# Loads and stores of 125 partitions issued as two, of 112 and 13, in a four-layer graph network on one core

## The chip, the cores and the metric

The kernel runs on one core of a Trainium2 chip. The metric is device time in microseconds (us): the median of several executions of the whole program. The profile is one further execution, recorded by the hardware profiler.

## What is computed

The reference applies four layers to x, 3125 nodes with 256 features each, on a graph with 103,125 directed edges (50,000 random pairs in both directions, and a loop at each node, sorted by target). Each layer is

```
xn = layernorm(x)
x = x + gnn(xn, edges) + mix(xn)
x = x + ffn(layernorm(x))          # layers 0, 2, 3 shown alike; layers 1 and 2 feed x itself
```

with other functions in each layer. Layers 0 to 2 use graph attention over (source, target) pairs alone and a linear attention over all nodes as mix. Three parts matter here:

- ffn of layer 0: a router picks the best 2 of 8 experts for each node; an expert is 256 -> 512 (gelu) -> 256; the node gets the two results weighted by a softmax over the two scores.
- gnn of layer 3: every edge has 16 features and a mask of 4 values, so the attention weight of an edge can't be found from its two nodes alone. A softmax over the edges of a target weights the source rows of 8 heads of 32.
- ffn of layer 3: H = gelu(x W1 + b1) with 1024 features, then the most likely of 8 experts, 1024 -> 256, weighted by its probability.

In the result all 3125 x 256 values of x are float32.

## The kernel before

**Layout.** Nodes are cut into NT = 25 tiles of TP = 125, because 3125 = 25 x 125. So x, xn and most tensors with a row for each node have 125 partitions ([125, 25, 256] for x), and so have the transfers that load or store them. Transposed copies (xT) and weights have 128 partitions. GROUPS cuts the 25 tiles in seven groups (4, 4, 4, 4, 3, 3, 3). DRAM tensors of the kernel's own hold what must be read in another order: seg_d, xn_d, y_d, tab (the node table), hid_d.

**Order of work.** Parts outside a `manual_schedule` are put in order by the framework's scheduler, from its own estimate of costs; inside one, TensorE (PE) and VectorE (DVE) keep the order of the code. That is so in the edge loop of layer 3 and in the expert loops of layers 0 and 3 (`edge_attention`, `routed0`, `routed3`). DMAs are issued from the queues of SyncE (SP), ScalarE (ACT) and, for gathers and scatters by index, GpSimd (POOL). Each queue runs in order, and an issue on ACT or POOL stands in line with that engine's computation.

**The start.** `run` loads x with one DMA (L2420), 3.2 MB. `begin_layer` takes the layernorm group by group (L608 to L614) and transposes. `prepare` finds, for each of 3125 target nodes, where its edges begin in a padded list: heads_i (L1342, each partition gets the same 3224 values of row_dst, 1.6 MB), five VectorE reductions over them that count the heads below the partition's first node (L1352, `at`), at_i (L1355), a gather of `segments` by at_i on POOL (L1358), arithmetic on it, and two stores to seg_d (`lo` at L1371, `key` at L1376). Beside it stand checks on the data: dst_i (L1344) and the work on it (dst_f, above, under: L1390 to L1399), and the largest and smallest attention scores (seven pairs of reductions, L1409 and L1410). Their product is `ok` (L1436), and the program branches on it (L2423): with this data it always goes into `layers`.

**Counts and layer 0.** `counts` reads seg_d back ten times as seg_in, 125 x 256 values (L1466), transposes each on TensorE (L1468) and copies it with ACT. From is_lo (L1473) on it builds one-hot matrices and multiplies them (L1501) into a matrix of edge counts. Pieces of layer 0's mix run in between: the addition of bproj to x on POOL (L1528), which the memset of v (L1538) follows, and p_ctx on TensorE (L1540), which reads v. Attention of layers 0 to 2 is then dense, over count tiles (L1670 on VectorE, L1719 and L1770 on TensorE). `gate0` stores the normed rows to xn_d by groups (L2295) and scores the experts. `route` (L2072 to L2143) sorts the pairs of node and expert into tiles of 128. `routed0` gathers xn_d by index (L2353), runs the experts and scatters the results to y_d (L2406); afterwards it loads y_d back, for each group once on SP into xn and once on ACT into xT (L2399, 14 loads, 6.4 MB), and adds each to x (L2401, 50 operations). The next layernorm (L608) follows.

**Layer 3.** `edge_attention` first makes the node table: for each tile TensorE projects, ACT copies to z_row (L1880), and a store of 144.5 KB goes to the table (L1883), 13 on SP and 12 on ACT. The edge loop then has 101 steps of 8 columns of 128 edges. A step loads row (the targets of its edges, the same 1024 int16 values for 125 partitions, 250 KB, L1915, 4 buffers), ef (L1917) and mask (L1919) on SP; gathers eight times 128 table rows by source on POOL (L1925, z_edge, 3 buffers, 806 gathers in all); compares row with the node numbers on VectorE (hot, L1938); sums the target's and the edge's term on TensorE (p_m, L1953), copied to m_sb by ACT (L1955); forms the weights (l, L1968; near_e by ACT, L1976; oh, L1980; z_edge times near_e, L1984) and sums the weighted rows on TensorE (p_acc, L1993). Pieces of layer 3's mix and, for tiles that are done (ENDS), `hidden3` are put between: it computes H and stores it to hid_d with x (L2203, on SP) and with each half row of H (hid_row, L2214, on ACT, 50 stores). `routed3` loads w_d, eight experts of 1024 KB with 128 partitions (L2229), routes, gathers hid_d (hid_tile, L2239), multiplies, scatters to y_d, and copies the first 3125 rows of y_d to `out` with two DMAs from DRAM to DRAM (L2269, one on SP, one on ACT).

The line numbers are those of the kernel before.

Of the kernel before, what the change touches and what calls it, by code (L numbers as in the profile page):

```python
# [21 lines left out]
P = 128  # L22
N = 3125
TP = 125
# [16 lines left out]
NR = EP // ROW  # L41
KEYS = HI * GN
PIECES0 = 107
SC = 8
# [3 lines left out]
HID = 1024  # L48
# [8 lines left out]
class Net:  # L57
# [499 lines left out]
    def setup_dense(self):  # L557
        nc = self.nc
        self.eps10 = self.const.tile([P, 1], F32, name="eps10")
        nc.vector.memset(self.eps10, 1e-10)  # L560
        self.heads = self.const.tile([P, P], F32, name="heads")
        nc.vector.memset(self.heads, 0.0)
        for h in range(4):
            nc.vector.memset(self.heads[32 * h:32 * h + 32, 32 * h:32 * h + 32], 1.0)

    def vec(self, pool, name, rows=C):

# [754 lines left out]
class Dense(Net):  # L1322
# [8 lines left out]
    def prepare(self, pool, xT):  # L1331
# [6 lines left out]
        with ExitStack() as s:  # L1338
            w = s.enter_context(tc.tile_pool(name="prep", bufs=1))
            ps = s.enter_context(tc.tile_pool(name="prepp", bufs=2, space=PSUM))  # L1340
            heads_i = w.tile([TP, NR], I32, name="heads_i")
            nc.sync.dma_start(heads_i, dview(ins["row_dst"], 0, [[0, TP], [1, NR]]))  # L1342
            dst_i = w.tile([P, NE], I32, name="dst_i")
            nc.scalar.dma_start(dst_i, ins["dst_t"])  # L1344
            heads = w.tile([TP, NR], F32, name="heads_f")
# [22 lines left out]
            digit = w.tile([TP, GN, SEG], I32, name="digit")  # L1368
            nc.vector.tensor_scalar(digit, seg[:, :, SEG:], 127, None, op0=OP.bitwise_and)
            nc.vector.tensor_copy(lo, digit)  # L1370
            nc.sync.dma_start(self.seg_d[0], lo)  # L1371
            nc.vector.tensor_scalar(digit, seg[:, :, SEG:], 7, None, op0=OP.logical_shift_right)
            nc.vector.tensor_copy(key, digit)
            nc.vector.scalar_tensor_tensor(key, key, float(GN), rel, op0=OP.mult, op1=OP.add)
            nc.vector.scalar_tensor_tensor(key, key, -127.0, own, op0=OP.add, op1=OP.mult)
            nc.sync.dma_start(self.seg_d[1], key)  # L1376

            found = w.tile([P, 2], F32, name="found")
            nc.vector.memset(found, 0.0)
# [63 lines left out]
    def counts(self, pieces):  # L1443


        nc, tc = self.nc, self.tc
        self.count_d = self.dram.tile([NS, P, N], U8, name="count_d")
        B = 10
        with ExitStack() as s:
            c = s.enter_context(tc.tile_pool(name="cnt", bufs=1))  # L1450
            w = s.enter_context(tc.tile_pool(name="cntw", bufs=2))
            wo = s.enter_context(tc.tile_pool(name="cnto", bufs=1))
            work = pieces(c, wo)
            by_edge = []
            with tc.tile_pool(name="cnti", bufs=1) as wi, tc.tile_pool(name="cntt", bufs=2, space=PSUM) as ps:
                for i, name in enumerate(("lo_t", "key_t")):
                    seg = self.seg_d[i]

                    R = 2 if i else 1
                    t = c.tile([P, NG, 2, R], BF16, name=name)  # L1460
                    for b in range(GN):
                        x = wi.tile([TP, SEG], F32, name="seg_in", bufs=2)
                        nc.sync.dma_start(x, seg[:, b, :])
                        p = ps.tile([P, 2, TP], F32, name="p_t")
                        for i in range(2):
                            nc.tensor.transpose(p[:, i, :], x[:, i * P:(i + 1) * P], self.ident[:TP, :TP])  # L1466
                        for r in range(R):
                            nc.scalar.activation(t[:, b * TP:(b + 1) * TP, :, r], p.rearrange("p i g -> p g i"), AF.Copy)  # L1468
                    by_edge.append(t)
            ps = s.enter_context(tc.tile_pool(name="cntp", bufs=3, space=PSUM))  # L1470
            lo_t, key_t = by_edge
            is_lo = c.tile([P, P, 2 * B], BF16, name="is_lo")
            nc.vector.tensor_copy(is_lo, self.iota[:, :, None].to_broadcast([P, P, 2 * B]))  # L1473
            KP = KEYS + KEYS % 2
            is_key = c.tile([P, KP], BF16, name="is_key")
            nc.vector.tensor_scalar(is_key, self.iota[:, :KP], -127.0, None, op0=OP.add)
            is_pair = is_key.rearrange("p (k r) -> p k r", r=2)
            stage = None
            done, steps = 0, -(-NG // B)
            for g0 in range(0, NG, B):  # L1480
                n = min(B, NG - g0)
                m = 2 * n
                lo = lo_t[:, g0:g0 + n].rearrange("p g i r -> p (g i r)")
                key = key_t[:, g0:g0 + n].rearrange("p g i r -> p (g i) r")
                oh_lo = w.tile([P, P, 2 * B], BF16, name="oh_lo")
                nc.vector.tensor_tensor(oh_lo[:, :, :m], lo[:, None, :].to_broadcast([P, P, m]), is_lo[:, :, :m], OP.is_equal)

                oh_key = w.tile([P, 2 * B, KP], BF16, name="oh_key")
                nc.vector.tensor_tensor(oh_key[:, :m].rearrange("p m (k r) -> p m k r", r=2),
                                        key[:, :, None, :].to_broadcast([P, m, KP // 2, 2]),  # L1490
                                        is_pair[:, None].to_broadcast([P, m, KP // 2, 2]), OP.is_equal)
                at = g0 * GN % 250
                if at == 0:
                    stage = w.tile([P, NS, 250], U8, name="stage")
                for u in range(0, n, 4):
                    m = min(4, n - u)
                    p = ps.tile([P, 4, KEYS], F32, name="p_cnt")
                    for g in range(m):
                        for i in range(2):
                            j = 2 * (u + g) + i  # L1500
                            nc.tensor.matmul(p[:, g, :], oh_lo[:, :, j], oh_key[:, j, :KEYS], start=(i == 0), stop=(i == 1))  # L1501
                    o = stage[:, :, at + u * GN:at + (u + m) * GN]
                    nc.scalar.activation(o.rearrange("p t (g d) -> p t g d", d=GN),
                                         p[:, :m, :].rearrange("p g (t d) -> p t g d", d=GN), AF.Copy)
                if at + n * GN == 250 or g0 + n == NG:
                    d0, nd = g0 * GN - at, at + n * GN
                    nc.sync.dma_start(self.count_d[:, :, d0:d0 + nd].rearrange("t p d -> p t d"), stage[:, :, :nd])
                while done < (g0 // B + 1) * PIECES0 // steps:
                    next(work, None)
                    done += 1  # L1510
            for _ in work:
                pass
# [346 lines left out]
    def edge_attention(self, x, xT, weights, pieces, then):  # L1859
# [10 lines left out]
        with ExitStack() as s:  # L1870
            with ExitStack() as s2:
# [4 lines left out]
                for t in range(NT):  # L1876
# [3 lines left out]
                    nc.scalar.activation(zh[:, :, :D], p[:, :C].rearrange("p (h d) -> p h d", h=H), AF.Copy)  # L1880
                    nc.vector.tensor_copy(rows[:, t, HW:], p[:, C:C + EC])
                    nc.vector.tensor_copy(er[:, t, :], p[:, C + EC:])
                    (nc.scalar if t % 2 else nc.sync).dma_start(table[t * TP:(t + 1) * TP, :], rows[:, t, :])  # L1883
            wz = s.enter_context(tc.tile_pool(name="eg", bufs=3))
            w = s.enter_context(tc.tile_pool(name="ew", bufs=2))
            wt = s.enter_context(tc.tile_pool(name="et", bufs=1))
# [25 lines left out]
            def load(i):  # L1912
                c0, n = steps[i]
                rows[i] = w.tile([TP, SC * P], I16, name="row", bufs=4)
                nc.sync.dma_start(rows[i], dview(dst_d, c0 * P, [[0, TP], [1, SC * P]]))  # L1915
                efs[i] = w.tile([P, 2 * P], F32, name="ef", bufs=4)
                nc.sync.dma_start(efs[i], ins["edge16_s"][i])  # L1917
                masks[i] = w.tile([P, SC, 4], F32, name="mask", bufs=5)
                nc.sync.dma_start(masks[i][:, :n, :], ins["edge4_t"][:, c0:c0 + n, :])  # L1919
# [234 lines left out]
    def hidden3(self, w, ps, x, xn, xT, t0, nt, weights, ones, hid_d):  # L2154


        nc = self.nc
# [42 lines left out]
        nc.vector.tensor_mul(one, one, prob)  # L2200
        share = w.tile([TP, 4], F32, name="share")
        nc.vector.tensor_reduce(share[:, :nt], one, AX.X, OP.add)
        nc.sync.dma_start(hid_d[t0 * TP:(t0 + nt) * TP, HID + 1:].rearrange("(t p) f -> p t f", p=TP), x[:, t0:t0 + nt, :])  # L2203
        yield
        for t in range(nt):
            for i in range(2):
# [4 lines left out]
                nc.scalar.activation(row[:, :512], p[:TP], AF.Copy)  # L2211
                if i:
                    nc.scalar.activation(row[:, 512:], share[:, t:t + 1], AF.Copy)
                nc.scalar.dma_start(hid_d[(t0 + t) * TP:(t0 + t + 1) * TP, i * 512:(i + 1) * 512 + i], row[:, :512 + i])  # L2214
                yield

    def routed3(self, ones, hid_d, out):
# [7 lines left out]
        with ExitStack() as s:  # L2225
# [39 lines left out]
                        products(j - 1)  # L2265

            for i, q in enumerate((nc.sync, nc.scalar)):
                a, b = i * 62 * 25, 62 * 25 if i == 0 else N
                q.dma_start(out[a:b, :].rearrange("(p t) f -> p (t f)", t=25), y_d[a:b, :].rearrange("(p t) f -> p (t f)", t=25))  # L2269

    def matrix_rows(self, pool, name):

# [11 lines left out]
    def gate0(self, ps, x, xn, xT, xn_d, gate, t0, nt):  # L2284
# [5 lines left out]
        with self.tc.tile_pool(name="gate", bufs=1) as w:  # L2290
            v = w.tile([TP, nt, E], F32, name="score")
            for a, na in GROUPS:
                if t0 <= a < t0 + nt:
                    self.layernorm_twice(xn, x, (a, na))
                    nc.sync.dma_start(xn_d.rearrange("(p t) f -> p t f", p=TP)[:, a:a + na, :], xn[:, a:a + na, :])  # L2295
                    for k in range(KC):
                        p = ps.tile([P, 4, P], F32, name="p_o").rearrange("p a b -> p (a b)")
                        for t in range(na):
# [34 lines left out]
    def routed0(self, x, xn, xT, xn_d, gate, weights):  # L2333
# [8 lines left out]
        with ExitStack() as s:  # L2342
# [51 lines left out]
            for t0, nt in GROUPS:  # L2394
                last = t0 if t0 + nt <= KC * N // C else 0
                back = xT.rearrange("p k n -> p (k n)")[:TP, last * C:(last + nt) * C].rearrange("p (t f) -> p t f", f=C)
                for i, y in enumerate((xn[:, t0:t0 + nt, :], back)):
                    own = y_d[i * N:(i + 1) * N, :].rearrange("(p t) f -> p t f", p=TP)
                    (nc.scalar if i else nc.sync).dma_start(y, own[:, t0:t0 + nt, :])  # L2399
                    for t in range(nt):  # L2400
                        nc.vector.scalar_tensor_tensor(x[:, t0 + t, :], y[:, t, :], share[:, i, t0 + t:t0 + t + 1], x[:, t0 + t, :],  # L2401
                                                       op0=OP.mult, op1=OP.add)
# [10 lines left out]
    def run(self, x_in, out):  # L2413
# [3 lines left out]
        x = pool.tile([TP, NT, C], F32, name="x")  # L2417
        xn = pool.tile([TP, NT, C], F32, name="xn")
        xT = pool.tile([P, KC, N], F32, name="xT")
        nc.sync.dma_start(x, x_in.rearrange("(t p) c -> p t c", p=TP))  # L2420
        out_v = out.rearrange("(t p) c -> p t c", p=TP)
        self.begin_layer(x, xn, xT)
        ok = nc.values_load(self.prepare(pool, xT)[0:1, 0:1], min_val=0, max_val=1)  # L2423
# [181 lines left out]
```

## Time and profile before

| | |
|---|---|
| median of 3 runs | 5643.09 us (5640.39 to 5653.39) |
| profiled execution | 5665.5 us, its span 5663.4 us |
| granted TensorE clock, mean | 0.931 |
| busy: PE, VectorE, ScalarE, GpSimd | 87%, 67%, 18%, 18% of the span |
| DMA | 395.78 MB, mean 70 GB/s over the span |

The profiled execution is one of its own and was 22 us longer than the median of the others; times of lines and stretches come from it. A busy share is a mean over stages with different limits: layers 0 to 2 (to about 4300 us) are dominated by VectorE's products (L1670, 1482 us in 1200 instructions) and TensorE's sums over them, the edge loop (4372 to 5430 us) by POOL, TensorE and VectorE side by side. In lists of groups, "out<-in" gives the tensors by the program's names, and "125x256 f32" partitions, elements and type. In a row by stretch of time the last columns are the clock granted to TensorE, the mean busy share of the core's 16 DMA engines and the rate in GB/s.

### The profile page before, as it was taken

What the parts mean: (1) busy time and instruction counts of PE and PEld (TensorE: products, weight loads), DVE (VectorE), ACT (ScalarE), POOL (GpSimd) and SP (SyncE); (2) the same over time, 40 slices, a digit from 0 to 9 for tenths busy, and PEclk for the clock granted to TensorE, in tenths of its full rate; (3) what the DMA queues carried; (4) which work ended last, traced back from release to release, by engine and by line L of the source; (5) the groups of instructions that cost most, each with busy time, mean ns of one, the idle gap of its engine ahead of it and who ended that gap; (6) DMA issues with size and microseconds to landing.
All of it is one profiled execution on the core that took longest, in us unless ns stands there. A gap on an engine that the chain in (4) does not pass through costs nothing. (4 is left out here: it accounts for less than half of the span.)

```text
span 5663.4 us, 66627 instructions
## 1 busy us (share of the span) xinstructions
PE 4906.3 (87%) x24880; PEld 2860.4 (51%) x24880; DVE 3770.6 (67%) x6022; ACT 1040.4 (18%) x1993; POOL 1036.5 (18%) x1183
## 2 busy tenths in 40 slices
PE   3988888879778899989999899979998778988868
PEld 1652234448645433368644433345565556555547
DVE  6789999975455599845443899932222887776743
ACT  1540010011132100110123100023232112332221
POOL 1000000004300000000001100000000777767733
PEclk7999999979889999999889999979999889999979
DMA  2462222232200011111000011020001556656655
GB/s 84 33 62 72 76 63 66 67 109 63 84 29 1 24 34 35 36 40 36 22 1 4 25 33 33 27 70 0 1 0 51 160 158 172 173 173 163 180 161 177
DMA packets 288899, 395.78 MB, mean 70 GB/s; under 512 B 118753, under 2 KB 222578, under 8 KB 287997
## 3 DMA queue, kind: packets, MB, share of 16 engines
q1 hardware_dynamic: 203926, 165.26, 12.0%
q0 software_dynamic: 52496, 167.11, 10.8%
q10 hardware_dynamic: 32148, 59.05, 3.2%
q8 instruction: 203, 3.33, 0.2%
q14 instruction: 126, 1.03, 0.1%
HBM read 345.14 MB, written 49.35 MB: 70 GB/s over the span
## 5 line engine op out<-in xcount | busy, mean ns | idle before, releaser
L1670 DVE SCALAR_TENSOR_TENSOR pt<-q_head,bar,a 128x750 f32<-128x750 f32 (+5 forms) x1200 | 1482.3, 1295 | 80.9 <-PE acc L1775 57.8
L1925 POOL DMA_INDIRECT z_edge<-tab,src_i x806 | 774.2, 961 | 284.0 <-issue 209.2
L1719 PE MATMUL acc<-pt,zs 128*64 128x500 f32 (+2 forms) x2800 | 592.3, 549 | 151.6 <-DVE pt L1670 151.3
L1993 PE MATMUL p_acc<-z_edge,oh 128*125 128x264 f32 x2044 | 539.5, 425 | 101.7 <-DVE z_edge L1984 101.6
L1770 PE MATMUL acc<-pt,zs 128*64 128x375 f32 (+2 forms) x3200 | 605.2, 501 | 25.3 <-DVE pt L1670 24.9
L1993 PEld LDWEIGHTS p_acc<-z_edge,oh 128*125 128x125 f32 x2044 | 418.8, 209 | 202.1 <-DVE z_edge L1984 112.8
L1719 PEld LDWEIGHTS acc<-pt,zs 128*64 128x64 f32 (+1 forms) x2800 | 244.9, 137 | 483.6 <-DVE pt L1670 327.7
L1770 PEld LDWEIGHTS acc<-pt,zs 128*64 128x64 f32 (+1 forms) x3200 | 245.1, 136 | 361.9 <-issue 224.7
L1186 DVE SCALAR_TENSOR_TENSOR x<-p_y,sm,x 125x256 f32<-125x256 f32 x200 | 93.8, 484 | 429.6 <-PE p_y L711 429.6
L1775 PE MATMUL acc<-pt,zs 128*32 128x375 f32 (+2 forms) x3200 | 313.4, 497 | 0.0
L1821 PE MATMUL acc<-zs,pt 128*125 128x257 f32 x1250 | 275.5, 383 | 11.7 <-issue 11.7
L1821 PEld LDWEIGHTS acc<-zs,pt 128*125 128x125 f32 x1250 | 234.7, 189 | 52.5 <-issue 14.5
L1984 DVE TENSOR_TENSOR z_edge<-z_edge,near_e 128x2112 f32<-128x2112 f32 (+1 forms) x101 | 236.4, 2341 | 18.6 <-ACT near_e L1976 18.5
L1181 ACT ACTIVATE h<-p_tr,bn 128x500 f32<-128x500 f32 (+1 forms) x224 | 161.5, 722 | 361.7 <-PE p_tr L711 361.7
L711 PE MATMUL p_y<-w_L_ffn_Wo,h 128*125 128x256 f32 x800 | 203.7, 387 | 0.0
L1670 DVE SCALAR_TENSOR_TENSOR pt<-q_all,bar,a 128x500 f32<-128x500 f32 (+3 forms) x175 | 118.9, 681 | 122.7 <-PE acc L1821 120.2
L711 PE MATMUL p_tr<-h,w_L_ffn_W 128*128 128x500 f32 (+1 forms) x448 | 192.7, 554 | 7.7 <-ACT h L1181 4.6
L1617 POOL MEMSET es<- 128x4 f32 (+2 forms) x4 | 1.4, 346 | 1053.7 <-PE acc L1775 725.2
L711 PE MATMUL p_tr<-xT,w_L_ffn_W 128*128 128x500 f32 (+1 forms) x448 | 193.9, 556 | 0.0
L2309 POOL CAST one_e<-one 125x96 bf16<-125x96 f32 (+1 forms) x2 | 2.1, 1050 | 1024.4 <-DVE one L648 1024.4
L1775 PEld LDWEIGHTS acc<-pt,zs 128*32 128x32 f32 (+1 forms) x3200 | 85.0, 109 | 203.1 <-issue 201.8
L711 PEld LDWEIGHTS p_y<-w_L_ffn_Wo,h 128*125 128x125 f32 x800 | 144.9, 187 | 73.5 <-ACT h L1181 27.2
(504 smaller groups left out, 7014.9 us busy)
## 6 DMA issues: line engine op xcount, KB each, us to landing
row<-dst_row SPq DMA_DIRECT2D x101, 250.0 KB
a<-count_d SPq DMA_DIRECT2D x96, 203.1 KB
a<-count_d SPq DMA_DIRECT2D x96, 187.5 KB
a<-count_d SPq DMA_DIRECT2D x144, 93.8 KB
ef<-in_edge_s SPq DMA_DIRECT2D x101, 128.0 KB
z_edge<-tab,src_i POOLq DMA_INDIRECT x806, 3.0
count_d<-stage SPq DMA_DIRECT2D x12, 781.2 KB
q_head<-q_g ACTq DMA_DIRECT2D x24, 375.0 KB
```

What stands on the lines that cost most here:

```text
L711: self.nc.tensor.matmul(p, a, b, start=(i == 0), stop=(i == len(pairs) - 1))
L1181: nc.scalar.activation(o[:, m, :n], p[:, :n], AF.Relu, bias=b[:, e, m:m + 1], scale=g[:, e, m:m + 1])
L1186: nc.vector.scalar_tensor_tensor(x[:, t0 + t, :], q, wf[:, t, e:e + 1], x[:, t0 + t, :], op0=OP.mult, op1=OP.add)
L1670: self.nc.vector.scalar_tensor_tensor(pt[:K, :n], q, bar, a[:K, :n], op0=OP.max, op1=OP.mult)
L1719: nc.tensor.matmul(acc[64 * i:64 * i + 64, :b1 - b0], zs[:K, t, z:z + 64], pts[i][:K, b0:b1], start=(t == 0), stop=(t == NS - 1))
L1770: nc.tensor.matmul(acc[i // 2][64 * (i % 2):64 * (i % 2) + 64, b, :b1 - b0], zs[:K, t, i * W:i * W + 64], pts[i][:K, b0:b1], **st)
L1775: nc.tensor.matmul(acc[2][32 * i:32 * i + 32, b, :b1 - b0], zs[:K, t, z:z + 32], pts[i][:K, b0:b1], **st)
L1821: nc.tensor.matmul(acc[i], pt[:K, i * TP:(i + 1) * TP], zs[:K, t, :C + 1], start=(t == 0), stop=(t == NS - 1))
L1925: nc.gpsimd.indirect_dma_start(out=zs[i][:, j, :], out_offset=None, in_=table, in_offset=bass.IndirectOffsetOnAxis(ap=src[:, c0 + j:c0 + j ...
L1984: nc.vector.tensor_mul(zh, zh, weight[:, :, :, None].to_broadcast([P, n, H, D + 1]))
L1993: nc.tensor.matmul(acc[t], ohs[i, t][:, k - a, :], zs[i][:, k - c0, :HW], start=(k == cols[t][0]), stop=(k == cols[t][1] - 1))
L2309: nc.gpsimd.tensor_copy(ones[:, 0, ts, :], one1)
```

## The change

A helper, `part_dma`, issues one transfer of 125 partitions as two on the same queue: partitions 0 to 111 and 112 to 124. It is used for the row heads, both stores to seg_d and the loads of seg_in, the stores of xn_d, the loads of y_d in `routed0`, the stores of the node table, the load of row in the edge loop, and the stores of hid_d. Besides: x is loaded by groups, alternately on SP and ACT (so its one DMA becomes 14); of the five pairs of seg_in loads for each of two tensors the second and the fourth go to ACT's queue instead of SP's; and the copies to `out` become two of 1536 rows (24 rows to a piece, 64 pieces) and one of the last 53 rows on POOL's queue, instead of 1550 and 1575 rows (62 and 63 pieces of 25).

```diff
+    def part_dma(self, queue, out, in_):
+
+        queue.dma_start(out[:112], in_[:112])
+        queue.dma_start(out[112:TP], in_[112:TP])
...
-            nc.sync.dma_start(heads_i, dview(ins["row_dst"], 0, [[0, TP], [1, NR]]))
+            self.part_dma(nc.sync, heads_i, dview(ins["row_dst"], 0, [[0, TP], [1, NR]]))
...
-            nc.sync.dma_start(self.seg_d[0], lo)
+            self.part_dma(nc.sync, self.seg_d[0], lo)
...
-            nc.sync.dma_start(self.seg_d[1], key)
+            self.part_dma(nc.sync, self.seg_d[1], key)
...
-                        nc.sync.dma_start(x, seg[:, b, :])
+                        self.part_dma(nc.scalar if b % 2 else nc.sync, x, seg[:, b, :])
...
-                    (nc.scalar if t % 2 else nc.sync).dma_start(table[t * TP:(t + 1) * TP, :], rows[:, t, :])
+                    self.part_dma(nc.scalar if t % 2 else nc.sync, table[t * TP:(t + 1) * TP, :], rows[:, t, :])
...
-                nc.sync.dma_start(rows[i], dview(dst_d, c0 * P, [[0, TP], [1, SC * P]]))
+                self.part_dma(nc.sync, rows[i], dview(dst_d, c0 * P, [[0, TP], [1, SC * P]]))
...
-        nc.sync.dma_start(hid_d[t0 * TP:(t0 + nt) * TP, HID + 1:].rearrange("(t p) f -> p t f", p=TP), x[:, t0:t0 + nt, :])
+        self.part_dma(nc.sync, hid_d[t0 * TP:(t0 + nt) * TP, HID + 1:].rearrange("(t p) f -> p t f", p=TP), x[:, t0:t0 + nt, :])
...
-                nc.scalar.dma_start(hid_d[(t0 + t) * TP:(t0 + t + 1) * TP, i * 512:(i + 1) * 512 + i], row[:, :512 + i])
+                self.part_dma(nc.scalar, hid_d[(t0 + t) * TP:(t0 + t + 1) * TP, i * 512:(i + 1) * 512 + i], row[:, :512 + i])
...
-                a, b = i * 62 * 25, 62 * 25 if i == 0 else N
-                q.dma_start(out[a:b, :].rearrange("(p t) f -> p (t f)", t=25), y_d[a:b, :].rearrange("(p t) f -> p (t f)", t=25))
+                a, b = i * 1536, (i + 1) * 1536
+                q.dma_start(out[a:b, :].rearrange("(p t) f -> p (t f)", t=24), y_d[a:b, :].rearrange("(p t) f -> p (t f)", t=24))
+            nc.gpsimd.dma_start(out[3072:N, :], y_d[3072:N, :])
...
-                    nc.sync.dma_start(xn_d.rearrange("(p t) f -> p t f", p=TP)[:, a:a + na, :], xn[:, a:a + na, :])
+                    self.part_dma(nc.sync, xn_d.rearrange("(p t) f -> p t f", p=TP)[:, a:a + na, :], xn[:, a:a + na, :])
...
-                    (nc.scalar if i else nc.sync).dma_start(y, own[:, t0:t0 + nt, :])
+                    self.part_dma(nc.scalar if i else nc.sync, y, own[:, t0:t0 + nt, :])
...
-        nc.sync.dma_start(x, x_in.rearrange("(t p) c -> p t c", p=TP))
+        x_v = x_in.rearrange("(t p) c -> p t c", p=TP)
+        for i, (t0, nt) in enumerate(GROUPS):
+            self.part_dma(nc.scalar if i % 2 else nc.sync, x[:, t0:t0 + nt, :], x_v[:, t0:t0 + nt, :])
```

## The prediction

> **What bounds the kernel now.** I read the page first, then busy time, granted clock and DMA share by stretches of time, then the timeline at each place where the diff touches a load, and last the waits of POOL. The page says that TensorE is busy for most of the span, so a faster transfer gains only where all engines stand and wait for it:
>
> ```profile
> PE 4906.3 (87%) x24880; PEld 2860.4 (51%) x24880; DVE 3770.6 (67%) x6022; ACT 1040.4 (18%) x1993; POOL 1036.5 (18%) x1183
> ```
>
> Three such places exist. The first two show in the stretches (columns: stretch, its length, busy us of PE, PEld, DVE, ACT, POOL, granted clock, DMA share, GB/s); the third row group is a load of 128 partitions for comparison:
>
> ```profile
> 10.00:20.00 10.00, 0.00 (x0) 0.00 (x0) 1.17 (x2) 0.00 (x0) 0.00 (x0) 1.00 0.34 121
> 20.00:26.00 6.00, 0.00 (x0) 0.00 (x0) 0.00 (x0) 0.00 (x0) 0.00 (x0) 1.00 0.34 121
> ...
> 1540.00:1550.00 10.00, 0.00 (x0) 0.00 (x0) 3.90 (x10) 0.00 (x0) 0.00 (x0) 0.50 0.32 132
> 1550.00:1560.00 10.00, 0.00 (x0) 0.00 (x0) 3.25 (x8) 0.00 (x0) 0.00 (x0) 0.50 0.32 131
> ...
> 5468.00:5472.00 4.00, 0.00 (x0) 0.00 (x0) 3.90 (x21) 0.60 (x1) 0.00 (x0) 0.50 1.03 375
> 5472.00:5476.00 4.00, 0.30 (x3) 0.43 (x4) 3.87 (x15) 0.00 (x0) 0.00 (x0) 0.50 1.07 386
> ```
>
> At 10 to 26 us x is loaded, at 1540 to 1560 the results y_d of layer 0's experts: both have 125 partitions, both keep the 16 DMA engines busy to 0.32 to 0.34, close to 5/16 = 0.31, and move 121 to 132 GB/s. The load of w_d, with 128 partitions, fills all of them and moves 375 to 386. In the first two places TensorE stands and VectorE works at most 4 of 10 us. The timeline (start, us, engine, line, operation, count, idle before and its releaser) shows where these waits end:
>
> ```profile
> 33.69 0.75 DVE L608 BATCH_NORM_STATS2 bn_st<-x 125x6 f32<-125x256 f32 x2 [22.50 <-DMA x<-in_x]
> ...
> 1538.97 1.67 DVE L2401 SCALAR_TENSOR_TENSOR x<-xn,share,x 125x256 f32<-125x256 f32 x4 [21.18 <-DMA xn<-y_d]
> ...
> 1585.16 0.75 DVE L608 BATCH_NORM_STATS2 bn_st<-x 125x6 f32<-125x256 f32 x2
> ...
> 4360.33 0.38 ACT L1880 ACTIVATE z_row<-p_z 125x256 f32<-125x256 f32 x1 [1.73 <-DMA tab<-z_row]
> ...
> 4371.64 0.25 SPq L1915 DMA_DIRECT2D row<-dst_row  x1
> ```
>
> VectorE starts on x at 33.69; the last x update of layer 0 ends at 1585; and after the last row of layer 3's node table (4360) nothing moves until its stores have landed (4371.6). Then the edge loop of layer 3 begins, over 1000 us that belong to POOL's gathers:
>
> ```profile
> L1925 POOL DMA_INDIRECT z_edge<-tab,src_i x806: 940/946/1947, 4372.4 to 5429.1; - x162
> ...
> POOL z_edge L1925 <- issue: 209.2, 686, 0.5
> POOL z_edge L1925 <- PE p_acc L1993: 49.5, 37, 6.2
> ```
>
> One gather is 0.946 us and 0.30 of issue, so 806 need 1.25 x 806 = 1007 of the 1058 us; 49.5 us are waits for a buffer that PE's sums free.
>
> **What the skill says.** "DMA: Bandwidth & Descriptors", section "Why a DMA increments its semaphore by 16 and not by 1": a hardware-issued DMA runs on k engines, k the largest number up to 16 that divides the outermost sizes of both sides. 125 gives 5, 112 gives 16, 13 gives 13. The trace agrees: 0.34 against 1.03 above. The same page, "Issuing engines are not separate dma queues": a second issuing queue saves only issue time. So the alternation of SP and ACT earns little by itself; the trace has 0.25 to 0.7 us for an issue. No page prices the waits that doubled DMAs bring.
>
> **The change, part by part.** After a split an engine carries at most 7 + 1 = 8 partitions instead of 25, so a lone transfer can be 3.1 times as fast, up to the 375 to 386 GB/s seen. Each split adds one issue of 0.25 to 0.4 us on its queue. The compiled order also shows that SP's and ACT's DMAs take eight semaphores in turn, and that a DMA waits for the one eight before it; twice the DMAs means half the reach.
>
> *Start.* x is 3.2 MB: 31 us at 121 GB/s and after the change about 10 at 325 (16 engines at the 20 GB/s that each shows here), but VectorE needs only the first groups. They land near 5.5 us (issue 0.7 to 2.5, then 1 MB of groups 0 and 1 mixed at 325 GB/s = 3.1). Groups then come every 1.5 us, while VectorE takes 25 us for seven. The row heads (1.6 MB, 5 us) follow at about 18 and are needed at 30. Before, VectorE worked from 33.69 to at_i at 78.2. The compiled order moves 4.6 us of dst work (L1390, L1397 to L1399, hidden under x until now, because dst_i's load sits behind x on ACT's queue and three activations) into this chain, and 2.3 us of reductions out of it: 5.5 + 44.5 + 4.6 - 2.3, with some waits 53.7, so at_i is 24.5 earlier. The gathers of segments and the work to seg_key take 12 + 13.7 us as before. But the compiled order puts six of seven pairs of L1409/L1410 behind seg_key, where only one was: with TensorE cold (0.8 us a matmul at first) I count 9 us, of which the seg_key store hid 2.6 before. So the branch comes near 95 instead of 110.9: **gain 15** (11 to 22; more if the reductions slip forward, less if the groups queue on each other).
>
> *Start of the counts.* Ten seg_in loads become twenty, four of them on ACT. Each transfer shrinks by under 1 us, but POOL's addition of bproj (L1528, 13.8 us, on which v's memsets and TensorE's p_ctx wait) now has its load behind a seg_in on ACT, and a waiting seg_in holds ACT's ek, v and key_t copies. **-1** (-5 to +4).
>
> *Stores of xn_d and of seg_d.* The last xn_d store is issued by 1241, the gather that reads it starts at 1278 behind the routing (L2072 to L2143): nothing; if that cover went, 3 us.
>
> *Results of layer 0.* 6.4 MB in 14 loads, and 2.6 MB of weights ahead of them on the same engines from 1518. At 350 GB/s 9.0 MB take 26 us, so the last lands near 1546. VectorE needs 50 x 0.41 = 20.5 us, from a first arrival near 1532: it ends at 1552 instead of 1585.2, and VectorE itself is late next. **Gain 32** (26 to 37; the low end is 300 GB/s and stalls on the eight semaphores).
>
> *Node table.* 25 stores, 3.6 MB, ran at 109 GB/s for 37 us against TensorE's 27. After the split TensorE paces them (1.08 us a tile, two stores each); the last is issued at 4360.1 and lands 2.5 later, as POOL's scatters do: 4362.7 instead of 4371.6. **Gain 8.5** (5 to 9.5).
>
> *Edge loop.* The loads of row (250 KB, 101 times) and the stores of hid_d (25.6 + 15.6 MB in all) lie on five engines that the gathers also need; spread out, a gather's worst landing (7.5 us, median 3.0) shrinks, and with it part of the 49.5 us. Against it: 50 more issues of 0.26 us on ACT, 110 on SP, which is idle. The trace doesn't show how much of the 49.5 is late landing: between 10 gained and 6 lost, **gain 4**.
>
> *End.* hid_d's last stores shared five engines with w_d; at 5476 to 5480 the rate dips to 159 GB/s. That is 1.3 MB lost, 3.5 us at 380: **gain 2.5** (0 to 4). The out copies are DRAM to DRAM and already fill the engines (378 to 411 GB/s, 10 us). Theirs shrink by 1 to 3%; the 53 rows on POOL (0.8 us issue, 2.5 landing) end under them: 0 (-0.5 to 0.5).
>
> Sum: 15 - 1 + 32 + 8.5 + 4 + 2.5 = 61 us. The work between these places is bound by TensorE and VectorE, in an order that the change leaves alone, so it shifts whole. The profiled execution had 5665.5 us (span 5663.4 and 2.1 around it), 22 above the median 5643.1; I take the 61 off both: 5604 there, **5582** as median.
>
> **Rivals.** (a) The engines double but not the rate: DRAM rows of 1 to 4 KB on 16 engines stay near 200 GB/s, or the eight semaphores let only two or three large transfers fly. Then y_d takes 45 us (gain 16), the start gains 8, the table 5: about 5613. For it: dips to 213 GB/s at 1526; against: 326 GB/s mean over 36 us around w_d, most of it 1 KB packets. (b) The edge loop was held by the five busy engines: 25 of the 49.5 us come back: 5558. For it: DVE waits 53.6 us for z_edge; against: gathers of 10.0 us a step leave little anyway. (c) Slower: in the edge loop ACT's hid_d stores wait for a semaphore held by an SP load that itself waits for a buffer, and near_e and m_sb queue behind them. It needs over 61 + 11 us in 101 steps, 0.7 us in each, to lose. For it: ACT runs in order; against: ACT is idle for 75% of this stage, and the load eight back was issued a step and a half earlier. Near 5660. (d) The split doesn't reach more engines: no change.
>
> **How the numbers follow.** Forecast 0.66, (a) 0.13, (b) 0.12, (c) 0.05, (d) 0.04. About 0.2% (11 us) is what a measurement of this kernel can tell from no change. Faster 0.92, the same 0.03, slower 0.05. The forecast's own bounds, added in squares, are about 14 us; with (a) and (b) the range is 5554 to 5610.
>
> **What would show it.** Right: VectorE's first L608 near 6 us and is_lo near 95; DMA share over 0.9 with 300 GB/s in the y_d loads, and these done within 30 us of their first issue; the row load of the edge loop 3 us after the last z_row; 806 gathers still in 1040 to 1060 us. Wrong: a share that stays at 0.33; SP or ACT queue waits on earlier DMAs between the halves; ACT late for near_e.

## The result and the profile after

The kernel after takes 5583.36 us (5581.36 to 5585.78, 4 runs), the kernel before 5648.24 us beside it (5640.39 to 5653.39, 4 runs): ratio 0.9885, 95% interval 0.9873 to 0.9897, faster by 65 us. The forecast was 5582. (Against 5643.09, the median of three runs of before from which the forecast started, it is 60 us; in two later sets of seven runs before had 5647.57 and 5643.06.) The profiled execution of after took 5581.4 us (span 5579.3) and lies near its median, whereas that of before was 22 us above its own, so a second profile of the kernel before (e1, below) is the better partner. The span cut at the same events in all three, in us:

| from one event to the next | before | before, second profile | after | second to after |
|---|---|---|---|---|
| start to is_lo (the branch is taken) | 110.9 | 110.5 | 93.9 | -16.6 |
| to the first count product | 35.8 | 36.6 | 37.4 | +0.8 |
| to the first y_d load | 1376.9 | 1365.7 | 1364.7 | -1.0 |
| to the last group of y_d additions | 61.2 | 61.0 | 38.1 | -22.9 |
| to the last z_row | 2775.5 | 2760.8 | 2762.1 | +1.3 |
| to the first gather of the edge loop | 12.1 | 12.2 | 3.5 | -8.7 |
| to the last gather | 1056.7 | 1063.3 | 1048.0 | -15.3 |
| to the copies to out | 221.1 | 221.0 | 214.4 | -6.6 |
| to the end | 13.2 | 13.3 | 17.2 | +3.9 |

The page of after has the same work on every engine; TensorE's share rises by a point only because the span is shorter:

```profile
PE 4887.1 (88%) x24880; PEld 2854.4 (51%) x24880; DVE 3778.7 (68%) x6022; ACT 1037.5 (19%) x1991; POOL 1038.3 (19%) x1184
```

Stretches of after, at the load of x and in the y_d loads (columns as in the prediction):

```profile
10.00:20.00 10.00, 4.52 (x24) 3.73 (x24) 10.00 (x48) 2.84 (x7) 0.00 (x0) 1.00 0.98 262
...
1512.00:1522.00 10.00, 0.00 (x0) 0.00 (x0) 6.76 (x18) 0.00 (x0) 0.00 (x0) 0.50 0.99 252
1522.00:1532.00 10.00, 0.00 (x0) 0.00 (x0) 9.32 (x24) 1.28 (x1) 0.00 (x0) 0.50 0.92 264
```

The engines' share tripled, from 0.32 to nearly 1.0, but the rate only doubled, from 131 to some 255 GB/s: 16 GB/s an engine where each of five gave 26. VectorE, which worked 3 to 4 us in ten during the y_d loads, now works 7 to 9.

The timeline of after where the waits end:

```profile
8.00 0.75 DVE L613 BATCH_NORM_STATS2 bn_st<-x 125x6 f32<-125x256 f32 x2 [6.33 <-DMA x<-in_x]
...
1509.59 0.88 DVE L2407 SCALAR_TENSOR_TENSOR x<-xn,share,x 125x256 f32<-125x256 f32 x2 [19.30 <-DMA xn<-y_d]
...
1533.29 1.27 DVE L2407 SCALAR_TENSOR_TENSOR x<-xT,share,x 125x256 f32<-125x256 f32 x3
...
4296.18 0.38 ACT L1885 ACTIVATE z_row<-p_z 125x256 f32<-125x256 f32 x1 [1.07 <-PE p_z L716]
...
4298.90 0.30 SPq L568 DMA_DIRECT2D row<-dst_row  x1
```

VectorE starts on x at 8.0 instead of 33.7. The y_d additions end 38.5 us after the first of their loads is issued (1496.0), not 61.6, and the row load follows the last z_row by 2.7 us, not 11.3. The gathers and POOL's waits in the edge loop of after:

```profile
L1930 POOL DMA_INDIRECT z_edge<-tab,src_i x806: 940/946/1949, 4299.7 to 5347.7; - x162
...
POOL z_edge L1930 <- issue: 207.9, 682, 0.5
POOL z_edge L1930 <- PE p_acc L1998: 40.9, 40, 5.3
```

A gather costs what it did, 0.946 us, with the same issue time; only the wait for p_acc fell, from 49.5 us (53.4 in the second profile of before). What stands ahead of p_acc's sums fell too: VectorE's wait, at its first product with a gathered row (l), for the gathers to land. In before, before again and after it was (total us, times, longest)

```profile
DVE l L1968 <- DMA z_edge<-tab,src_i: 53.6, 21, 6.8
DVE l L1968 <- DMA z_edge<-tab,src_i: 83.1, 26, 7.1
DVE l L1973 <- DMA z_edge<-tab,src_i: 36.0, 14, 6.2
```

In the set of measurements in which e5 to e8 ran, the kernel before had a median of 5938 us and the edge loop took 1335 to 1351 us in all four kernels, 393 to 412 us of it in waits of ACT before m_sb that are put to events outside the core; the cause stays open, so only their other stages are compared.

### The profile page after: what moved, and what is told of

The parts are those of the page before. It is cut to its first block, busy times and chain, and to the rows that moved or that the text cites. A ratio compares the mean times of both kernels' runs of the same rounds, so it can differ in the third digit from the quotient of the medians.

```text
span 5579.3 us, 66975 instructions
## 1 busy us (share of the span) xinstructions
PE 4887.1 (88%) x24880; PEld 2854.4 (51%) x24880; DVE 3778.7 (68%) x6022; ACT 1037.5 (19%) x1991; POOL 1038.3 (19%) x1184
## 5 line engine op out<-in xcount | busy, mean ns | idle before, releaser
L1191 DVE SCALAR_TENSOR_TENSOR x<-p_y,sm,x 125x256 f32<-125x256 f32 x200 | 93.9, 484 | 428.2 <-PE p_y L716 428.2
```

Of the source, the lines that this page charges most:

```text
L1191: nc.vector.scalar_tensor_tensor(x[:, t0 + t, :], q, wf[:, t, e:e + 1], x[:, t0 + t, :], op0=OP.mult, op1=OP.add)
```

## The experiments

**e1: the kernel before, once more.** No edit.

> The kernel before, unchanged, profiled once more: it gives a second set of stage lengths. Two stages that the change was not expected to touch were shorter in the profile after: from the first count product to the first y_d load (1376.9 us before, 1364.7 after) and from the end of the y_d additions to the last z_row (2775.5 before, 2762.1 after), together 25.6 us. Theory 1, those are differences between executions (the first profile of before was 22 us above the median): this run has a time near 5645 and the two stages together at least 12 us shorter than in the first profile. Theory 2, the change shortens them: they repeat within 4 us, 1377 and 2775. The stages that hold the changed transfers (start 111, y_d 61, table 12) repeat within 1 us in both.

5646.5 us; the two stages came to 1365.7 and 2760.8, together 25.9 us below the first profile. Theory 1 holds: the change has no part in them. The stretches from the y_d additions to the node table, of before, of before again and of after, show what differs:

```profile
1585.00:4360.00 2775.00, 2619.33 (x12512) 1396.95 (x12512) 1625.89 (x3068) 507.69 (x963) 50.40 (x88) 0.95 0.08 22
```

```profile
1574.00:4334.00 2760.00, 2605.70 (x12512) 1390.06 (x12512) 1626.07 (x3068) 508.08 (x963) 50.50 (x88) 0.96 0.08 23
```

```profile
1534.50:4296.00 2761.50, 2609.75 (x12509) 1392.13 (x12509) 1625.64 (x3067) 507.63 (x963) 50.48 (x88) 0.96 0.08 23
```

The number of products is the same, VectorE's time is the same, and PE's busy time is 14 us longer in the first, where the granted clock was 0.95 and not 0.96. The other kernels go with that: at 0.95 this stage took 2770.9 and 2771.1 us (e9, e12), at 0.96 2758.5 to 2767.7 (e3 apart, 2778.0). So a profile's span can be some 20 us off with the clock; the stages that hold the changed transfers repeated within 1 us outside the edge loop.

**e2: the split at 120 and 5; e3: at 124 and 1.** As after, with as many DMAs.

```diff
-        queue.dma_start(out[:112], in_[:112])
-        queue.dma_start(out[112:TP], in_[112:TP])
+        queue.dma_start(out[:120], in_[:120])       # e3: 124
+        queue.dma_start(out[120:TP], in_[120:TP])   # e3: 124
```

> As after, but every split is 120 and 5 instead of 112 and 13. In after the y_d loads kept the DMA engines busy to 1.0 at only 245 to 275 GB/s, 16 GB/s an engine, where five engines gave 25 each before. Theory 1, seven partitions to an engine do not fall on whole groups of partitions[...]; eight to an engine (15 engines) do, like w_d's 128: the y_d stage shrinks from 38 to about 30 us, the rate goes to 320 GB/s or more, the whole kernel 5 to 10 us faster. Theory 2, the rate is held by something that the split does not change (source rows in DRAM, two queues at once): y_d stage 38 to 41, rate 235 to 270, time within 5 us of after. Both: first layernorm near 8 us, table stage 3.5.

5584.74 us (ratio to before 0.9907, 0.9877 to 0.9937); y_d stage 39.5 us, as theory 2 had it.

> As after, with as many DMAs, but every split is 124 and 1. Theory 1, the number of engines is the largest divisor up to 16 of the partitions, so 124 gives 4: transfers at about 100 GB/s, below the 125 of before. Then the y_d stage is 75 us (61 before, 38 after), the table stage 13 (12, 3.5), the start about 105 (111, 94; the groups of x still help), the edge loop no shorter than before, and the whole is at or above the time before: 5640 to 5680. Theory 2, two DMAs in flight instead of one, or shorter ones, give the gain: 5575 to 5595, stages as after.

5704.1 us (ratio 1.0103, 1.0084 to 1.0123), 56 us slower than before and more than I had allowed. The stages: start 125.5 (105 expected), y_d 73.4 (75), table 8.9 (13), gathers 1077.2. Stretches of the y_d loads in e3 and in e2:

```profile
1550.00:1560.00 10.00, 0.00 (x0) 0.00 (x0) 3.47 (x9) 0.00 (x0) 0.00 (x0) 0.50 0.26 105
1560.00:1570.00 10.00, 0.00 (x0) 0.00 (x0) 3.35 (x8) 0.00 (x0) 0.00 (x0) 0.50 0.26 106
```

```profile
1524.30:1533.30 9.00, 0.00 (x0) 0.00 (x0) 8.76 (x23) 1.28 (x1) 0.00 (x0) 0.50 0.90 244
```

124 partitions fill 0.26 of the engines, near 4/16, and move 105 GB/s, less than one DMA of 125 did. So the two DMAs are not what gains; the number of engines is, and the divisor sets it. 120 partitions (15 engines, eight to each) are no better than 112 (16, seven to each): my reason for the low rate, seven to an engine, falls. In e3's edge loop VectorE's wait for gathers is the longest of all kernels compared there, 91.8 us.

**e4: y_d loads whole.**

```diff
-                    self.part_dma(nc.scalar if i else nc.sync, y, own[:, t0:t0 + nt, :])
+                    (nc.scalar if i else nc.sync).dma_start(y, own[:, t0:t0 + nt, :])
```

> As after, but the 14 loads of y_d are whole again (125 partitions). My account: the y_d stage goes back from 38 to 61 us, the time to about 5606, 23 more than after, all else as after. Rival, the order of instructions that the scheduler chose for the begin of layer 1 (it differs with these loads) carries part of the difference: then the stage from the end of the y_d additions to the last z_row goes back as well, from 2762 towards 2775, and the time to 5618.

5608.04 us (ratio 0.9932, 0.9913 to 0.9951), 24.7 above after; the y_d stage is 61.8 us and the stage behind it 2762.7. The split of y_d is worth 23 to 25 us, and the order of the instructions that follow nothing.

**e5: y_d loads of 128 partitions.**

```diff
+        nc.sync.dma_start(y_d[2 * N:2 * N + 3 * NT, :], xn_d[:3 * NT, :])
...
-                    own = y_d[i * N:(i + 1) * N, :].rearrange("(p t) f -> p t f", p=TP)
-                    self.part_dma(nc.scalar if i else nc.sync, y, own[:, t0:t0 + nt, :])
+                    own = y_d[i * N:i * N + P * NT, :].rearrange("(p t) f -> p t f", p=P)
+                    (nc.scalar if i else nc.sync).dma_start(y, own[:, t0:t0 + nt, :])
```

> As after, but the y_d loads take 128 partitions in one DMA (xn's tile has 128 partitions, and the views of y_d run 75 rows past each result; 75 rows of y_d are filled beforehand by a copy, so that they hold numbers; partitions 125 to 127 are not used). Theory 1, only a transfer of all 128 partitions[...]: the rate rises from 250 to above 330 GB/s as for w_d, the y_d stage falls from 38 to about 30 us, the time to about 5575. Theory 2, the rate is set by the rows or by loads from two queues at once, or by the weights that go before: rate 240 to 275 with the engines full, stage 36 to 39, time as after, 5583. Theory 3, the number of DMAs in flight (eight semaphores) starves the engines: half the DMAs give a stage of 33 to 35.

The y_d stage took 32.9 us, nearest to theory 3, but the rate speaks for the first (stretches of e5's y_d loads):

```profile
1508.50:1514.50 6.00, 0.00 (x0) 0.00 (x0) 0.00 (x0) 0.00 (x0) 0.00 (x0) 0.50 1.03 358
1523.50:1531.50 8.00, 0.00 (x0) 0.00 (x0) 8.00 (x21) 1.28 (x1) 0.00 (x0) 0.50 1.00 370
```

With the engines as full as in after they move 358 to 370 GB/s; where transfers were lacking, in after from 1505 to 1508 us, the share fell with the rate, to 0.43 and 132 GB/s. e5 also has one DMA in place of two for each load, so whether it is the 112 or the 13 beside them that lowers the rate is not separated. The whole took 5880.11 us (ratio 0.9905, 0.9872 to 0.9938), an interval too wide to show 5 us. In the second row of the stretches VectorE is busy without a gap: the additions have become the bound, which is why the stage stops at 33. The Trainium skill, "SBUF — State Buffer", section "Door 1: The DMA port swizzle (why `[64,N]` ≈ `[32,N]`)", says that the memory has 16 ports for DMAs, each for eight partitions that don't lie together, and that in a transfer of 128 partitions each engine serves one port. That would explain why only 128 reaches the full rate, but the runs here show rates, not ports: 105 GB/s for 124 and 1, 131 for 125, 244 for 120 and 5, 252 to 264 for 112 and 13, 358 to 370 for 128.

**e6 and e7: the queue of y_d, grouping against splitting of x, the queue of the last rows.** Two edits each, in stages far apart.

```diff
-                    self.part_dma(nc.scalar if i else nc.sync, y, own[:, t0:t0 + nt, :])
+                    self.part_dma(nc.sync, y, own[:, t0:t0 + nt, :])                                             # e6
...
-            self.part_dma(nc.scalar if i % 2 else nc.sync, x[:, t0:t0 + nt, :], x_v[:, t0:t0 + nt, :])
+            (nc.scalar if i % 2 else nc.sync).dma_start(x[:, t0:t0 + nt, :], x_v[:, t0:t0 + nt, :])   # e6
+        self.part_dma(nc.sync, x, x_v)                                                                # e7, no loop
...
-            nc.gpsimd.dma_start(out[3072:N, :], y_d[3072:N, :])
+            nc.sync.dma_start(out[3072:N, :], y_d[3072:N, :])                                         # e7
```

> Two edits in stages far apart. (1) All y_d loads are issued on SP (112 and 13 as in after). Theory 1, two queues at once slow the packets: stage 30 to 34 us instead of 38, rate over 320. Theory 2, the queue doesn't matter: 38 to 41. (2) x comes by groups on SP and ACT as in after, but each group whole, 125 partitions. Theory A, the number of engines is what gains at the start: first layernorm near 8 us, but the groups land at 121 GB/s until 33 us and the row heads after them, at_i at 66 to 70 (54 in after, 78 before). Theory B, the grouping alone gives it: at_i at 54 to 58.

> Two edits in stages far apart. (1) x in one piece of 112 and one of 13 partitions on SP, no groups. Theory A (engines): x lands near 12 us, at_i at 57 to 61, branch near 97 (54 and 94 in after). Theory B (groups): first layernorm near 12, at_i at 66 or later. (2) The last 53 rows of the output on SP's queue instead of POOL's. In after the stage from the first out copy to the end is 17.2 us, 13.2 before, though the data ended after 10 in both. Theory A, a transfer issued by POOL at the end costs about 4 us of closing: the stage goes back to 13 to 14. Theory B, a third transfer, or one on few engines, costs it: 17.

e6 took 5894.16 us and e7 5882.99, one run each; only their stages are read. In e6 the y_d loads from one queue moved 259 GB/s with the engines full:

```profile
1527.00:1537.00 10.00, 1.72 (x8) 1.15 (x7) 10.00 (x28) 0.30 (x1) 0.00 (x0) 0.50 1.02 259
```

The queue doesn't matter to the rate. (Its stage was 49.2 us because the scheduler put layernorms of layer 1 between the additions, another order, not slower data.) The stretches of e6 in its load of x:

```profile
6.00:12.00 6.00, 0.00 (x0) 0.00 (x0) 1.00 (x4) 0.00 (x0) 0.00 (x0) 1.00 0.34 120
12.00:18.00 6.00, 0.00 (x0) 0.00 (x0) 2.30 (x12) 0.00 (x0) 0.00 (x0) 1.00 0.34 121
```

Groups without the split leave the rate at 121; at_i comes at 66.2 and is_lo at 106.3. So of the 16.6 us of the start 4 are there with x in whole groups (the row heads and seg_d split), and splitting x brings the rest. The split without groups (e7) has at_i only at 63.7, between the two theories and 9.5 after that of after, for x lands at 19.8; yet is_lo comes at 95.3, 1.4 later. That is the scheduler's order: the 4.6 us of dst work had gone back under the load of x (dst_f at 7.1, in after at 36.1), and behind seg_key stood one of the seven pairs of reductions for the largest and smallest scores, as in before, where after has six (80.2 to 90.2). With the last rows on SP the closing took 13.4 us.

**e8: row and hid_d whole; e9: the old copies to out; e10: row whole; e11: hid_d whole.** In each, the named `part_dma` is again one `dma_start` on the same queue; e9 is

```diff
-                a, b = i * 1536, (i + 1) * 1536
-                q.dma_start(out[a:b, :].rearrange("(p t) f -> p (t f)", t=24), y_d[a:b, :].rearrange("(p t) f -> p (t f)", t=24))
-            nc.gpsimd.dma_start(out[3072:N, :], y_d[3072:N, :])
+                a, b = i * 62 * 25, 62 * 25 if i == 0 else N
+                q.dma_start(out[a:b, :].rearrange("(p t) f -> p (t f)", t=25), y_d[a:b, :].rearrange("(p t) f -> p (t f)", t=25))
```

> As after, but the row loads of the edge loop and the stores of hid_d are whole again. Theory 1, five busy engines held up the gathers: the stage of the gathers goes from 1048 to 1057 to 1063 us (before), that from the last gather to the out copies from 214 to 221, and the time from 5583 to 5598 to 5604. Theory 2 (my estimate on record, the loop gains 4): the gathers take 1052, the end 217, the time 5590. Rival, none of it: the loop's difference is only spread between executions, 1048 and 5583.

> As after, but the output is copied as in before (1550 and 1575 rows on SP and ACT, none on POOL). Theory 1, the closing after a transfer that POOL issued costs some 4 us: the stage from the out copies to the end is 13.2 to 13.5 us (17.2 in after), the time 5579. Rival, the closing is long for another reason (one of the kernels with POOL's transfer had 13.8): 15 to 17. This run is also the stand-in for after beside the two that follow: gathers 1047 to 1051 us, last gather to out copies 214.

> As after, but the 101 loads of row in the edge loop are whole (125 partitions, 25 MB on five engines); the stores of hid_d stay split. Theory R, these loads held up the gathers' landings: the stage of the gathers rises by 8 to 13 us over the kernel with all split (to 1056 to 1063), from the last gather to the out copies unchanged, 214; the time 8 to 13 us above after. Theory H, the stores of hid_d did: gathers 1047 to 1051, time as after.

> As after, but the 57 stores of hid_d are whole (15.6 MB on five engines); the loads of row stay split. Theory R, the gathers are as in after (1047 to 1051) and only the end is longer, 221 instead of 214 us from the last gather to the out copies, since the last stores share five engines with w_d: time 7 us above after. Theory H, the gathers take 1056 to 1063 as well, time 15 to 20 above after. My estimate on record for the end was 2.5 us, which would show as 216 to 217.

Stages in us. For e9 to e11 the kernel before had a median of 5643.06 beside them:

| | gathers | last gather to out | out to end | time | ratio to before |
|---|---|---|---|---|---|
| all split, old out (e9) | 1050.2 | 214.8 | 13.3 | 5578.73 | 0.9884 (0.9867 to 0.9900) |
| row whole (e10) | 1051.9 | 213.3 | 17.3 | 5584.32 | 0.9892 (0.9876 to 0.9909) |
| hid_d whole (e11) | 1055.8 | 218.6 | 13.9 | 5582.70 | 0.9892 (0.9875 to 0.9908) |
| both whole (e8, loop not comparable) | - | 221.7 | 13.8 | 5880.57 | 0.9901 (0.9877 to 0.9926) |
| both whole (before, twice) | 1056.7, 1063.3 | 221.1, 221.0 | 13.2, 13.3 | | |

Kernels with all split gathered in 1047.2 to 1050.8 us (after, e2, e4, e9). Row whole is 1 us beyond that band, hid_d whole 5 us, each in one profile, where before itself differs by 7 us between two. Theory R's 1056 to 1063 did not come with row whole; theory H's came within 0.2 us with hid_d whole, though not its 15 to 20 us in the time. That points to the stores of hid_d more than to the larger loads of row, but does not prove it. The waits of e9, e10 and e11, in this order, show a part for both:

```profile
DVE l L1973 <- DMA z_edge<-tab,src_i: 47.3, 17, 6.8
DVE l L1973 <- DMA z_edge<-tab,src_i: 56.2, 19, 6.8
DVE l L1973 <- DMA z_edge<-tab,src_i: 61.5, 22, 7.2
```

VectorE waits for gathers 9 us longer than in e9 with row whole and 14 us with hid_d whole. POOL's wait for p_acc rises less, 43.1, 45.4 and, in e11,

```profile
POOL z_edge L1930 <- PE p_acc L1998: 49.0, 43, 6.4
```

which is that of before (49.5). At the end hid_d whole costs 4 us. The two whole together cost 6 to 16 us in the loop and 7 at the end; that the parts add up is not shown, and the times, whose intervals all overlap, don't part these kernels. e8, which was to test both at once, could do so only at the end, where it has the 221 us of before.

The closing: without a transfer on POOL it is 13.2 to 13.4 us in before, e7 and e9 and 14.1 in e12; with it 16.9 to 17.4 in after, e2, e3, e4, e6 and e10, but 15.6 in e5 and 13.8 to 13.9 in e8 and e11. POOL's transfer alone does not explain it, nor do fewer DMAs on ACT's queue (e4 and e5 have equally many there, at 17.3 and 15.6). What decides is not settled.

**e12: 128 wherever the source allows it.** y_d as in e5, row, row_dst and six of the seven groups of x with 128 partitions in one DMA, stores split as in after, out as in before.

```diff
-                self.part_dma(nc.sync, rows[i], dview(dst_d, c0 * P, [[0, TP], [1, SC * P]]))
+                nc.sync.dma_start(row, dview(dst_d, c0 * P, [[0, P], [1, SC * P]]))   # rows[i] = row[:TP]
...
+            if t0 + nt < NT:
+                q.dma_start(x_all[:, t0:t0 + nt, :], dview(x_in, t0 * TP * C, [[C, P], [TP * C, nt], [1, C]]))
```

> What the runs so far suggest: loads of 128 partitions in one DMA wherever the source allows it (y_d as in the run before on this; row, row_dst; x by groups, whose last group stays 112 and 13), stores split 112 and 13, and the output copied as in before. y_d stage 33 us (38 in after), start 92 to 94 (94), gathers 1044 to 1050, the end 13.3 instead of 17.2: time 5570 to 5577 against 5583 of after. If one DMA in place of two gives nothing in the edge loop, the gain is 9; if the loop gains from fewer waits on semaphores, up to 14. Rival, what y_d gains is given back by another order of instructions at the begin of layer 1: 5579.

5580.91 us (5577.04 to 5585.07), ratio 0.9887 (0.9871 to 0.9904): not to be told from after. Its loads of x show the rate of 128 partitions a second time, with rows of 1 KB where y_d has rows of 3 and 4 (e12, then after, from 4 to 12 us):

```profile
4.00:12.00 8.00, 1.41 (x6) 1.09 (x7) 6.68 (x32) 1.00 (x3) 0.46 (x8) 1.00 1.09 383
4.00:12.00 8.00, 0.00 (x0) 0.00 (x0) 4.00 (x21) 1.58 (x2) 0.45 (x8) 1.00 1.09 273
```

The share is the same, the rate 383 against 273 GB/s. The stages are as expected where data was late (y_d 32.8, start 92.2) but the gathers stayed at 1051.7, the closing took 14.1 and not 13.3, and the stage behind y_d, in this execution 2771.1, varies by more than what is left to gain.

## Why the prediction was right, step by step

The total, 61 us forecast and 65 measured, is right for the reason given, and the waits went at the three places named; but that it is so close is partly luck, for errors cancel: y_d brought 9 us less, the edge loop 5 to 11 more, the end 4 more, the copies to out 4 less.

- **Start: right.** 15 forecast, 16.6 measured, by the steps named: at_i at 54.2 (53.7 forecast), is_lo at 93.9 (95), the dst work moved into the chain (dst_f at 36.1) and six pairs of reductions behind seg_key, 10 us of them where 9 were counted. VectorE's first L608 came at 8.0, not 5.5, yet at_i only 0.5 late.
- **Start of the counts: not decided**, a loss of 0.8 us (1 forecast), within the spread of this stage (36.9 to 40.0 in e9 to e12). **Stores of xn_d and seg_d: right**, no change beyond the spread of the clock.
- **Results of layer 0: too high, and outside its bounds.** 32 forecast (26 to 37), 23 measured. The step that failed is "At 350 GB/s 9.0 MB take 26 us" and, with it, the "first arrival near 1532", 8 us after the first issue. The rate was taken from w_d, a load of 128 partitions, for a transfer of 112 and 13, which gets 252 to 264 with full engines. The first tile arrived 13.6 us after its issue, and VectorE waited another 4.5 us later. e5 parts the two: at 358 to 370 GB/s its stage is 5 us shorter, but its first tile still takes 12.0 us (issued at 1505.45),

```profile
1517.49 0.88 DVE L2408 SCALAR_TENSOR_TENSOR x<-xn,share,x 125x256 f32<-125x256 f32 x2 [17.88 <-DMA xn<-y_d]
```

because some 4 MB had moved by then (an estimate from the rates of e5's stretches), where 8 us at 350 are 2.8. So about half of the error is the rate and the rest what shares the engines ahead of the first tile. Rival (a) had the engines without the rate. Its first reason, short rows, did not hold: rows of 1 to 4 KB move at 358 to 383 GB/s with 128 partitions. Its second, too few transfers in flight, seems to hold for a short while in after: the sign that the prediction named for being wrong is there, SP's second half waiting for an earlier DMA, a load of layer 1's parameters, and soon after it the engines run low:

```profile
SPq L569 <- DMA r_L_mix_g<-in_L_mix_g: 4.9, 1, 4.9
1505.00:1508.00 3.00, 0.00 (x0) 0.00 (x0) 0.00 (x0) 0.00 (x0) 0.00 (x0) 0.50 0.43 132
```

In that stretch the engines are not even half busy; from 1514 on they are full, and the rate is still near 250.

- **Node table: right.** 8.5 forecast, 8.7 measured; the row load came 2.7 us after the last z_row began (2.4 forecast).
- **Edge loop: too low.** 4 forecast (to 10), 9 or 15 measured against the two profiles of before. The sign was right, and so was the mechanism as far as the waits show it: VectorE waited 36.0 us for gathers where before had 53.6 and 83.1, and POOL 40.9 us for p_acc. Single landings were not measured after the change. The size was not to be had from one profile, since the loop of before itself differs by 7 us between executions. Rival (b) asked for 25.
- **End: too low.** 2.5 forecast (0 to 4), 6.6 measured. The term priced only the dip in the rate of w_d; e11 puts 4 us of it to the stores of hid_d, and the rest stays open.
- **Copies to out: wrong.** Forecast 0, "the 53 rows on POOL end under them". Their data does, but the closing of the program, which was put at nothing, became 3.9 us longer. With the old copies (e9) or the 53 rows on SP (e7) it is short again, 13.3 and 13.4; the cause stays open, since e11 keeps POOL's transfer and has 13.9.
- **Rival (c)**, ACT held by DMAs, didn't appear: the loop became shorter.

## What to carry to other kernels

Count the engines of a transfer from the largest divisor up to 16 of its partition count (124, 125, 120 and 112 partitions showed shares of 0.26, 0.32, 0.90 and 0.92 to 0.99 here, for 4, 5, 15 and 16 of 16 engines), and look at share and rate together: a share of 5/16 with nothing else running is time to be had, but a full share at 250 GB/s is not yet the full rate, which came only with 128 partitions (y_d in e5, x in e12, w_d). A load that may read a few rows past its end, or a broadcast, can simply take 128; a store of 125 can't. For the loads of y_d the split gave about half of what was missing (131, 252 to 264, 358 to 370 GB/s); for the node table's stores it cut the wait from 12.1 to 3.5 us. Transfers on few engines also go with longer waits beside them: VectorE waited for the edge loop's gathers 36 to 48 us where row and hid_d were spread over 15 or 16 engines, 54 and 83 in before (five) and 92 in e3 (four). Price the gain at the places where all engines wait, and stop where the next engine takes over: at the y_d loads, VectorE's 50 additions left 5 us for a faster load to gain.

## What was not expected of the hardware

- 120 partitions on 15 engines (244 GB/s) move no faster than 112 on 16 (252 to 264), while 128 move 358 to 370: engines and bytes per engine don't set the rate alone.
- A split into 124 and 1 is worse than none: 105 GB/s against 131, and 56 us on the whole kernel.
- The last stage, from the issue of the copies to out to the end, took 13 to 17 us, of which the data took 10, with no pattern that one edit explains.
